# Two transformer layers on one core: the ends of pairs of query tiles start with the sums of their last exponentials

## The chip, the cores and the metric

The kernel runs on one core of one Trainium2 chip. It works with TensorE (PE), VectorE (DVE), ScalarE (ACT), GpSimd (POOL) and the DMA queue of SyncE (SP). The metric is the device time of one launch in microseconds (us), lower is better. Five runs of the kernel before gave 570.61 us in the median (563.48 to 572.50). The profile is of one other execution, which took 571.08 us.

## The reference

There are four batches of 512 tokens with 128 features, and four stages, each with a residual sum and a layer norm behind it:

```python
x = _layernorm(x + _L0_attn_ref(x, ...))   # 8 heads of 16, relative positions, softmax
x = _layernorm(x + _L0_ffn_ref(x, ...))    # 8 experts of 128->512->128, top 1, silu
x = _layernorm(x + _L1_attn_ref(x, ...))   # convolution, gates, scan over the sequence
x = _layernorm(x + _L1_ffn_ref(x, ...))    # 14 experts of 128->256->128, top 1, gelu
```

Of the first stage, this is what the change moves: the head outputs are divided by the sums of the exponentials, joined, and multiplied with Wo.

```python
attn = jax.nn.softmax(score, axis=-1)
ctx = jnp.einsum('bhqk,bkhd->bqhd', attn, v).reshape(b, s, e)
return ctx @ Wo + bo
```

The expert layers need the whole of their batches first: every token is given to the expert with the highest logit, tokens are sorted into blocks of 128 of one expert, and the blocks go through the matmuls. That sorting is done on the chip.

## The kernel before, in words

**Attention** is a list `steps` (L1327) of 64 steps (batch b, query tile t, pair of heads p), 16 to a batch. In turn k of `attention` (L1338) the scores of step k are computed (`main`, `aux`) and their row maxima taken on DVE (`nmax`); the exponentials of step k-1 (`pr`) run on ACT, which also sums them into `sums` (`exponentials`, L987); the exponentials of step k-2 are turned by PE (`ptr`) and copied by ACT (`prT`); and, in every second turn, four heads of step k-3 are multiplied with the values (`values`, L1011: `ctx`, copied to `cT`). So there are three turns behind the last scores, k = 64, 65 and 66, which only finish.

**Side work.** At the end of each turn the generators in the list `side` are advanced twice each, all of them once and then all again: the preparation of later batches (`attn_prep`), the ends of query tiles, and the first expert layer of batches 0 and 1 (`experts`, group 0). `pause(n)` (L404) lets 2n of these advances pass. `bank` (L410) makes a generator wait until the turn has a PSUM bank left for side work: `room` is 1 in turns with a `ctx`, otherwise 2. The order of instructions on every engine in this part is the order in which they are written.

**The end of two query tiles**, `tiles_end` (L1023), takes the reciprocal of the sums (`rec`), spreads it (`wide`), turns it on PE (`prr`), multiplies the head outputs with it (`cT`), multiplies with Wo on PE (`po`) and adds to the residual `xs`. It is entered into `side` in the turn in which the last `ctx` of its two tiles was issued, three turns behind their last scores. Behind the second pair of a batch, `attn_end` (L1056) takes over for the batch: moments, the reciprocal root (`rstd_b`, a power on POOL), `xf`, its transpose (`pxf`, `xfT`), the router (`pl`, `route` L524), the ranks of the tokens (`rank`, `dispatch` L606), and four indirect DMAs per batch from POOL that put the rows into `sent`. When both batches of a group are through, `experts` (L1086) fetches them (`rows`, on SP), turns them (`pxs`), and runs blocks through up matmuls (`ph`), bias and activation (`hb`, `th`) and down matmuls (`py`); the results go through DRAM (`ys`, `made`) and are gathered by POOL (`back`).

**Behind the attention** a planner takes over: `play` (L376) writes the instructions of many generators in the order in which a clock of estimated durations finds them ready, so one shift changes the order of all that follows. Where that clock sees PE idle for more than two microseconds, it puts in matmuls whose results are overwritten (L1676, `pass_time` L97). Two generators begin: `rest_of_last` (L1654), with priority, does the last `tiles_end` (batch 3, second pair) and the `attn_end` of batch 3, and then the experts of group 1 (batches 2 and 3); `rest_of_first` (L1639) finishes what is left in `side`, the `attn_end` of batch 2 and the experts of group 0. Then come the recurrences of the second layer (`pj`, `pg`, `pa`, `pgo`), its router, and its experts, first for group 0, then for group 1.

Of the kernel before, what the change touches and what calls it, by code (L numbers as in the profile page):

```python
# [19 lines left out]
B, S, D = 4, 512, 128  # L20
H, DH = 8, 16
# [177 lines left out]
def tile_kernel(ctx: ExitStack, tc: tile.TileContext, x, wpack, cols, rows, tabs, b2bd0, b2bd1,  # L199
# [37 lines left out]
    def ps(name):  # L237
        t = psum.tile([P, 512], F32, tag="any", name=name)
        clock.unread.add(clock.tile_of(t))
        clock.banks[clock.tile_of(t)] = t  # L240
        return t
# [34 lines left out]
    def col(name, i=0):  # L276
        at = _COLS[name][0] + i
        return colt[:, at : at + 1]
# [89 lines left out]
    def done():  # L368

        return clock.last  # L370
# [33 lines left out]
    def pause(n):  # L404

        if now[0] is not None:
            for _ in range(2 * n):
                yield

    def bank(*needs):  # L410
        if psum_e is not None:
            yield (*needs, common_bank)
            return
        while now[0] is not None and not room[0]:
            yield
            yield
        room[0] -= 1
# [569 lines left out]
    def exponentials(b, t, p, main, nmax):  # L987

        nm = f"{b}_{t}_{p}"
        if t % 2 == 0 and p == 0:  # L990
            sums[b, t // 2] = small.tile([P, 2, H], F32, tag="sums", bufs=2, name=f"sums{nm}")
        prs = []
        for i in range(2):
            pr = ap6.tile([P, S], F32, tag="pr", name=f"pr{nm}_{i}")
            nc.scalar.activation(pr, main[:, i, :], AF.Exp, bias=nmax[:, i : i + 1],
                                 accum_out=sums[b, t // 2][:, t % 2, 2 * p + i : 2 * p + i + 1])
            prs.append(pr)
        return prs

    def flip(b, t, h, pr):  # L1000
        nm = f"{b}_{t}_{h}"
        ptr = ps(f"ptr{nm}")
        for c in range(NT):
            nc.tensor.transpose(ptr[:, c * P : (c + 1) * P], pr[:, c * P : (c + 1) * P], ident)
        prT = ap6.tile([P, NT, P], F32, tag="prT", name=f"prT{nm}")
        nc.scalar.copy(prT.rearrange("p c q -> p (c q)"), ptr)
        return prT

    cTs, sums = {}, {}
# [13 lines left out]
    def tiles_end(b, t2):  # L1023

        nm = f"{b}_{t2}"
        cT = cTs.pop((b, t2))
        rec = small.tile([P, 2 * NG * 4], F32, tag="rec", bufs=1, name=f"rec{nm}")
        nc.vector.reciprocal(rec, sums.pop((b, t2)).rearrange("p i h -> p (i h)"))
        wide = ap2.tile([P, 2 * NG, 4, 2 * DH], F32, tag="wide", bufs=1, name=f"wide{nm}")
        nc.vector.tensor_copy(wide.rearrange("p g h d -> p (g h) d"), rec.unsqueeze(2).to_broadcast([P, 2 * NG * 4, 2 * DH]))  # L1030
        yield from pause(1)
        yield from bank(wide)
        pr_ = ps(f"prr{nm}")
        for g in range(2 * NG):
            nc.tensor.transpose(pr_[:, g * P : (g + 1) * P], wide[:, g].rearrange("p h d -> p (h d)"), ident)
        yield (done(),)
        flat = cT.rearrange("p i g q -> p (i g q)")
        nc.vector.tensor_tensor(flat, pr_, flat, ALU.mult)
        yield
        yield from bank(cT)  # L1040
        po = ps(f"po{nm}")
        for i in range(2):
            for g in range(NG):
                nc.tensor.matmul(po[:, i * D : (i + 1) * D], lhsT=cT[:, i, g, :], rhs=wwo[:, g, :],
                                 start=(g == 0), stop=(g == NG - 1))
        yield (done(),)
        mine = xs[b][:, 2 * t2 : 2 * t2 + 2, :].rearrange("p n d -> p (n d)")
        nc.vector.tensor_tensor(mine, po[:, : 2 * D], mine, ALU.add)
        if t2 == 1 and b < B - 1:
            gen = attn_end(b)  # L1050
            side.insert(0, gen)
            if b == GROUPS[0][-1]:
                urgent.append(gen)
        yield

    def attn_end(b):  # L1056

        last = b == B - 1
        x1[b] = keep.tile([P, NT, D], F32, tag="x1", name=f"x1_{b}")
        yield  # L1060
        mean, var = moments(xs[b], f"b{b}")
        rstd, both = yield from rstds_of(var, 1e-6, f"b{b}", nc.vector if last else nc.gpsimd)
        yield
        yield
        xf = keep2.tile([P, NT, D], F32, tag="xf", bufs=len(GROUPS[0]), name=f"xf{b}")
        xf_of[b] = xf
        apply_norm(xf, xs[b], mean, both, nc.vector)
        apply_norm(x1[b], xs[b], mean, rstd, nc.gpsimd)
        yield from pause(1)
        yield from bank(xf)  # L1070
        pt = transposed(xf, f"pxf{b}")
        yield (done(),)
        xfT[b] = keep2.tile([P, S], F32, tag="xfT", name=f"xfT{b}")
        nc.scalar.activation(xfT[b], pt, AF.Identity, scale=col("rms_w"))
        yield from pause(1)
        yield
        w = []
        yield from route(xfT[b], colr("gate"), E0, b, 0, w)
        if b == GROUPS[0][-1]:
            side.append(experts(0, 0, pack[0], E0, F0, "b1_0", col("rms_w")))  # L1080
        if last:
            begin(b2_of(w[0], b2t0, b, 0, x1[b], x1[b]), 1)
        else:
            yield from b2_of(w[0], b2t0, b, 0, x1[b], x1[b])
# [242 lines left out]
    steps = [(b, t, p) for b in range(B) for t in range(NT) for p in range(H // 2)]  # L1327

    side, urgent = [], []

    def advance(gens):
        for gen in list(gens):
            if next(gen, "end") == "end":
                gens.remove(gen)

    mains, probs, flipped, peaks = {}, {}, {}, {}

    def attention(first, last):  # L1338

        for k in range(first, last):  # L1340
            now[0] = k
            turning = [(*steps[k - 2], i) for i in range(2)] if 2 <= k < len(steps) + 2 else []

            def turn_one(b, t, p, i):
                flipped[b, t, 2 * p + i] = flip(b, t, 2 * p + i, probs[k - 2][i])


            if turning:
                turn_one(*turning[0])
            if k - 1 in peaks:  # L1350
                probs[k - 1] = exponentials(*peaks.pop(k - 1))
            if k < len(steps):
                mains[k] = scores(*steps[k])
                b, t, p = steps[k]
                if k == 3:
                    later_constants()
                    side.extend([turn_keys(), conv_weights(), clear_sent(), attn_prep(1), pack_weights()])
                if t == NT - 1 and p == 0 and b + 2 < B:
                    side.append(attn_prep(b + 2))
            if turning:  # L1360
                turn_one(*turning[1])
            due = None
            if 3 <= k < len(steps) + 3:
                b, t, p = steps[k - 3]
                if p % 2 == 1:
                    due = b, t, p // 2
                    values(*due, [flipped.pop((b, t, 4 * (p // 2) + i)) for i in range(4)])
            room[0] = (3 if k < 3 else 2) if due is None else 1
            if k < len(steps):
                peaks[k] = softmax(*steps[k], *mains.pop(k))  # L1370
            halves = list(side)
            advance(side)
            for gen in halves:
                if gen in side and next(gen, "end") == "end":
                    side.remove(gen)
            if due is not None and due[2] == 1 and due[1] % 2 == 1:
                side.insert(int(side[:1] == urgent), tiles_end(due[0], due[1] // 2))

    def wide_ps(name):
        if psum_e is None:  # L1380
# [273 lines left out]
    def rest_of_last():  # L1654
        last_experts = experts(1, 0, pack[0], E0, F0, "b1_0", col("rms_w"))
        next(last_experts)
        yield from tiles_end(B - 1, 1)
        yield from attn_end(B - 1)
        yield from last_experts
        load_layer1()  # L1660
        while 1 not in gxs:
            yield BLOCKED
        backs = []
        for b in GROUPS[1]:
            yield (made[0, 1], lambda: clock.free["gpsimd"])
            backs.append(gather(b, 0))
        for b, back in zip(GROUPS[1], backs):
            yield from layer0_end(b, back)
        for b in GROUPS[1]:
            while b - 2 not in over_with:  # L1670
                yield BLOCKED
            begin(recurrence(b), -1)
        yield from layer1(1)
# [114 lines left out]
```

## Time and profile before

| what | value |
|---|---|
| median of five runs | 570.61 us (563.48 to 572.50) |
| profiled execution: time, span | 571.08 us, 569.4 us |
| PE busy | 482.8 us, 85% of the span |
| DVE busy | 374.4 us, 66% |
| ACT busy | 297.5 us, 52% |
| POOL busy | 166.8 us, 29% |
| attention, from the first scores to the last `ctx` | 17.7 to 310.9 us |
| from there to the first rows of group 1 on PE | 310.9 to 349.5 us |
| recurrences and the rest of the first expert layer | 349.5 to 475.2 us |
| experts of the second layer, group 0 and then group 1 | 475.2 to 569.4 us |

Times within the span count from its first instruction. A line of the timeline reads: start, duration, engine, line, operation, tile written <- tiles read, shape, count, and in brackets the engine's idle time before it and what ended it. Nearly all operations have the line of one helper, L193, so tiles tell them apart. The profile counts two for each float32 matmul and one for each transpose, so a group written as four matmuls shows as x8 and four transposes as x4.

### The profile page before, as it was taken

The numbers are of one execution on the slowest core, as the hardware profiler recorded it, in microseconds if no ns is written. First come the engines' busy times: TensorE is split into PE (matmuls) and PEld (weight loads), VectorE is DVE, ScalarE is ACT, GpSimd is POOL, SyncE is SP. The second block draws the span as 40 slices with busy tenths as digits, with TensorE's granted clock in tenths as the row PEclk, the third lists the DMA queues.
The fourth block names the chain that finished last, engine by engine and source line by source line (L and its number), as shares of the span: only waits on it lengthen the run. The fifth ranks groups of instructions, "written<-read, shape, count | busy, mean of one in ns | idle before, by whom it ended". The sixth has DMA issues, their size and how long they took to land.

```text
span 569.4 us, 11328 instructions
## 1 busy us (share of the span) xinstructions
PE 482.8 (85%) x4076; PEld 338.6 (59%) x4076; DVE 374.4 (66%) x1033; ACT 297.5 (52%) x747; POOL 166.8 (29%) x272
## 2 busy tenths in 40 slices
PE   8988899988799888998897788999899897895930
PEld 5456465666556655676676665885445447794830
DVE  3777776776767866677573874964877586570615
ACT  1157566575655754566665121564563645573831
POOL 2484060140621402004000436313432222232533
PEclk9989999998999995699999989999999988897975
DMA  8999661330002800100328618751000017146432
GB/s 301 322 317 260 178 121 28 49 85 1 15 7 47 269 2 23 54 16 1 115 84 293 230 45 274 267 149 52 18 1 6 14 37 204 35 107 195 126 96 56
DMA packets 63848, 64.04 MB, mean 112 GB/s; under 512 B 4784, under 2 KB 53296, under 8 KB 63536
## 3 DMA queue, kind: packets, MB, share of 16 engines
q1 hardware_dynamic: 61744, 59.12, 35.6%
q0 software_dynamic: 2048, 4.20, 2.5%
q8 instruction: 32, 0.52, 0.4%
q14 instruction: 24, 0.20, 0.1%
HBM read 44.16 MB, written 20.45 MB: 113 GB/s over the span
## 4 chain that ended last, share of the span: by engine, by line
PE 53%; DVE 22%; ACT 9%; DMA 6%; issue 5%; POOL 3%; SPq 0%; ACTq 0%; DVEq 0%; POOLq 0%
PE ptr L193 8%; PE pa L193 7%; PE main L193 6%; PE ph L193 5%; PE py L193 5%; DVE nmax L193 4%; PE ctx L193 4%; DVE hb L193 4%; PE aux L193 4%; DVE main L193 3%; PE pj L193 3%; ACT pr L193 3%; ACT prT L193 2%; DMA rows<-sent 2%; PE pqa L193 1%
## 5 line engine op out<-in xcount | busy, mean ns | idle before, releaser
L193 ACT COPY prT<-ptr 128x512 f32<-128x512 f32 x128 | 74.6, 586 | 72.3 <-PE ptr L193 71.6
L193 PE MATMUL ptr<-ident,pr 128*128 128x128 f32 x512 | 86.2, 295 | 16.2 <-ACT prT L193 8.0
L193 PEld LDWEIGHTS ptr<-ident,pr 128*128 128x128 f32 x512 | 58.2, 147 | 56.1 <-ACT prT L193 17.8
L193 ACT ACTIVATE pr<-main,nmax 128x512 f32<-128x512 f32 x128 | 87.1, 689 | 6.5 <-DVE nmax L193 6.5
L193 DVE TENSOR_REDUCE nmax<-main 128x2 f32<-128x1024 f32 x64 | 78.4, 1224 | 2.2
L193 DVE COPY_PREDICATED main<-low,aux 128x256 f32<-128x256 uint32 x64 | 27.4, 428 | 64.1 <-PE aux L193 60.4
L193 PE MATMUL ph<-xt,wd 128*128 128x128 f32 x296 | 40.4, 280 | 7.9 <-ACT prT L193 4.8
L193 POOL DMA_INDIRECT back<-made,at x32 | 33.3, 1041 | 43.7 <-DMA made<-ys 23.6
L193 PE MATMUL aux<-Ko,QLo 32*128 32x128 f32 x472 | 44.5, 308 | 1.4 <-DVE mv_a L193 1.4
L193 PEld LDWEIGHTS ph<-xt,wd 128*128 128x128 f32 x296 | 36.1, 192 | 11.8 <-ACT prT L193 6.7
L193 PE MATMUL main<-KR,QR 32*128 32x512 f32 (+3 forms) x192 | 41.6, 511 | 0.0
L193 PE MATMUL ctx<-prT,V 128*32 128x128 f32 x1024 | 37.6, 292 | 4.6 <-ACT prT L193 3.8
L193 ACT ACTIVATE th<-hb 128x512 f32<-128x512 f32 x30 | 18.8, 629 | 38.7 <-DVE hb L193 36.2
L193 PEld LDWEIGHTS ctx<-prT,V 128*32 128x32 f32 x1024 | 28.0, 116 | 11.3 <-ACT prT L193 6.3
L193 PE MATMUL py<-wd,hb 128*128 128x128 f32 x248 | 32.1, 278 | 2.4 <-ACT prT L193 1.2
L193 PEld LDWEIGHTS aux<-Ko,QLo 32*128 32x128 f32 x472 | 32.9, 196 | 1.9 <-DVE mv_a L193 1.9
L193 PEld LDWEIGHTS py<-wd,hb 128*128 128x128 f32 x248 | 29.7, 192 | 5.1 <-ACT prT L193 1.6
L193 POOL DMA_INDIRECT sent<-x,at x16 | 17.2, 1072 | 47.3 <-ACT gKR L193 20.2
L193 PE MATMUL main<-K,QL 32*128 32x128 f32 (+2 forms) x192 | 29.5, 384 | 0.0
L193 POOL DMA_INDIRECT sent<-xf,at x16 | 16.3, 1016 | 43.5 <-DVE at L193 29.4
L193 DVE COPY_PREDICATED main<-ident,aux 128x256 f32<-128x256 uint32 (+1 forms) x64 | 27.4, 428 | 2.2
L193 DVE SCALAR_TENSOR_TENSOR res<-back,share,res 128x128 f32<-128x128 f32 x16 | 5.6, 351 | 34.8 <-DMA back<-made,at 34.8
(306 smaller groups left out, 991.8 us busy)
## 6 DMA issues: line engine op xcount, KB each, us to landing
wd<-pack SPq DMA_DIRECT2D x24, 512.0 KB, 5.4
wd<-pack SPq DMA_DIRECT2D x20, 256.0 KB, 3.7
pack<-in_W_dram SPq DMA_DIRECT2D x16, 256.0 KB, 5.7
rows<-sent SPq DMA_DIRECT2D x16, 256.0 KB, 3.7
made<-ys SPq DMA_DIRECT2D x16, 256.0 KB, 2.5
pack<-in_W_dram SPq DMA_DIRECT2D x28, 128.0 KB, 3.2
sent<-zero SPq DMA_DIRECT2D x2, 1344.0 KB, 11.0
tab<-in_tabs_dram SPq DMA_DIRECT2D x2, 1280.0 KB, 9.4
```

What stands on the lines that cost most here:

```text
L193: return inner(*args, **kw)
```

## The change

`tiles_end` is entered into `side` two turns earlier: at the end of the turn in which the exponentials of its last step were issued (k - 1), when `sums` is complete but the last `prT` and `ctx` are not. Its pause grows by one turn, and the head outputs are taken from `cTs` behind the pause. So `rec` and `wide` move two turns forward, `prr`, `po` and all that follows one turn. For batch 0's first pair it goes to the end of the list (it stands behind the preparation of batch 1), otherwise to its front as before. In the turns 64 to 66 only generators named `tiles_end` are advanced; the rest of `side` waits for the planner. `rest_of_last` takes up the last `tiles_end` where it stands in `side`, instead of beginning a new one.

```diff
     def tiles_end(b, t2):
         nm = f"{b}_{t2}"
-        cT = cTs.pop((b, t2))
         rec = small.tile([P, 2 * NG * 4], F32, tag="rec", bufs=1, name=f"rec{nm}")
...
-        yield from pause(1)
+        yield from pause(2)
+        cT = cTs.pop((b, t2))
         yield from bank(wide)
...
-    def advance(gens):
-        for gen in list(gens):
-            if next(gen, "end") == "end":
-                gens.remove(gen)
...
-            halves = list(side)
-            advance(side)
-            for gen in halves:
+
+            halves = [gen for gen in side if k < len(steps) or gen.__name__ == "tiles_end"]
+            for gen in (*halves, *halves):
                 if gen in side and next(gen, "end") == "end":
                     side.remove(gen)
-            if due is not None and due[2] == 1 and due[1] % 2 == 1:
-                side.insert(int(side[:1] == urgent), tiles_end(due[0], due[1] // 2))
+
+            if 1 <= k <= len(steps) and steps[k - 1][1] % 2 == 1 and steps[k - 1][2] == H // 2 - 1:
+                b, t, _ = steps[k - 1]
+                side.insert(len(side) if b == 0 and t == 1 else int(side[:1] == urgent), tiles_end(b, t // 2))
...
-        yield from tiles_end(B - 1, 1)
+        for gen in side:
+            if gen.__name__ == "tiles_end":
+                yield from gen
         yield from attn_end(B - 1)
```

## The prediction

> **What bounds the kernel now.** I read the page first (busy shares and the clock row), then the windows, then PE's timeline behind the attention, then the chain of waits. PE is busy 85% of the span, but the stages differ. In the attention a plain pair of turns takes 5.36 us (3.21 with a `ctx`, 2.15 without): ACT alone needs 5.0 of it (four `pr` at 0.69, four `prT` at 0.57). From 350 to 463 us PE has work nearly all the time: its named waits there sum to 7 us. Between lies this stretch, from PE's timeline (start, duration, tile, idle time before it):
>
> ```profile
> 312.78 0.66 PE L193 MATMUL prr<-ident,wide 128*128 128x128 f32 x4 [0.35 <-DVE hb L193]
> ...
> 322.77 0.60 PE L193 MATMUL pxf<-ident,xf 128*128 128x128 f32 x4
> ...
> 329.48 0.96 PE L193 MATMUL pl<-colt,xfT 128*128 128x8 f32 x8
> ...
> 333.90 0.36 PE L193 MATMUL rank<-before,ones 128*128 128x8 f32 x2 [0.67 <-DVE sm L193]
> ...
> 337.25 11.02 PE L1676 MATMUL pxs<-b2t,ident 128*128 128x512 f32 x18 [0.90 <-DVE farther L193]
> 349.51 0.66 PE L193 MATMUL pxs<-ident,rows 128*128 128x128 f32 x4 [1.24 <-DMA rows<-sent]
> ```
>
> These are batch 3's own steps; all group 1 waits for them. The last `ctx` ends at about 310.84. From there to the first rows of group 1, 38.7 us pass, and 12.3 of them (337.25 to 349.51) hold on PE only filler matmuls and idle time. The chain of waits names the end of it:
>
> ```profile
> 342.41 4.06 DMA sent<-xf,at
> 346.49 2.98 DMA rows<-sent
> 349.51 0.67 PE pxs L193 x4
> ```
>
> The second place is the clock. The windows (span, then busy us of PE, PEld, DVE, ACT, POOL, then granted clock) show a half clock that covers 213.6 to 237.5 us:
>
> ```profile
> 209.00:212.00 3.00, 2.12 (x19) 1.83 (x16) 2.76 (x7) 1.16 (x4) 0.00 (x0) 1.00 0.00 0
> 215.00:218.00 3.00, 2.21 (x34) 1.66 (x35) 2.73 (x13) 0.61 (x2) 0.00 (x0) 0.50 0.00 0
> ...
> 233.00:236.00 3.00, 3.00 (x9) 1.81 (x10) 2.71 (x6) 0.59 (x1) 0.00 (x0) 0.50 0.00 0
> 239.00:242.00 3.00, 3.00 (x50) 2.11 (x43) 1.88 (x3) 2.25 (x6) 0.00 (x0) 1.00 0.01 3
> ```
>
> Four turns take 24.0 us there (212.5 to 236.5); the same four of the batch before took 18.9 with 2.8 us more side work on PE. So this stretch costs 5 to 8 us, and five runs of one program that spread by 9 us may differ by just that.
>
> **The change part by part.**
>
> *Ends of tiles inside the attention.* Nothing is added or removed. `prr` (0.5 us issue) leaves a turn with `ctx` for one without, `po` (0.9) the reverse. A turn with `ctx` and `prr` takes 3.71, so +0.5 over plain; one with `po` and 1.1 of other work 4.41, +2.26 over 2.15 for 2.0 of work. The swap costs nothing to within 0.3 us for each of seven ends, so -2 to +2 in all; I take 0. `rec` and `wide` (0.25 + 0.43 on DVE) move ahead of two turns; the sums are there, since ACT issued those exponentials a turn before. DVE queues the next turn's masks and `nmax` behind them as it does now. POOL's clears of `V` and `QR` for a later batch and SP's copies of `QL` and `K` move by a turn or two, with ten turns to spare.
>
> *Group 0's experts start two turns earlier* (first `pxs` before turn 51, then 49), since batch 1's end comes earlier. By the order of instructions, one up, two downs and one `pxs` more then lie before the end of turn 63: 0.9 + 1.8 + 0.3 = 3.0 us of PE work. The twelve turns 51 to 62 took 55.6 us where plain ones take 32.2, for 14.65 us of side matmuls, so side work costs 1.6 us for each us on PE. That makes +4.8.
>
> *The last three turns* lose one up, `pxs`, two downs, and an up behind the last `ctx`. They took 10.6 us (300.25 to 310.84). What is left: `ptr` 0.6, `prT` 0.6, four `pr` pieces 1.35, `prT` 0.5, `ctx` 1.05, `cT` 0.3, `ptr` 0.7, two `prT` 1.05, 0.6 of hand-overs to PE: 6.8. So -3.8. The attention ends at +1.0 (from -1 if the early experts hide in ACT's shadow, to +2.5).
>
> *Batch 3's chain*, in us from the end of the last `ctx`, before in brackets. `prr` 0 (1.94: it stood behind an up and `pxf`, and waited for `hb`). `cT` times `prr` done at 1.45, `po` ends 2.6, `xs` starts 2.65 (5.28: DVE did batch 2's routing first). Moments take 1.74 as now: 4.4; the power on POOL 1.66: 6.15. Meanwhile DVE routes batch 2 (1.9 + 0.55), until 6.9; then root 0.82, `xf` 1.12: 8.85 (11.72). `pxf` and `xfT`: 10.4. `pl` follows at once, 11.4 (it ends at 19.6 now, because `xfT` stood on ACT behind a `th`, then `pl` on PE behind ups and downs). DVE then has batch 2's dispatch 2.3, `x` 0.6, `hb` 0.6 and 0.65, so `mx` starts at 13.1 and ends its group at 15.0 (22.8). `rank` 15.2 to 15.9. Ahead of the dispatch DVE has four `hb` pieces and the shares: 18.1; its 3.44 us end at 21.55 (27.36). Gain 5.8. POOL: the four `x` (3.31) now precede batch 2's four `sent` (5.0), 7.75 to 16.3, then the clear of `w` by 16.5; DVE needs that `w` at 16.75, so it is covered by a quarter of a us only. From dispatch to rows I keep the 11.2 us of now; on SP nothing that waits longer stands ahead of the rows. First rows of group 1: 349.5 + 1.0 - 5.8 = 344.7, a gain of 4.8 (bounds 2.3 to 7).
>
> *Behind it* the planner's order decides. Group 0's last results come 2.3 us later (its last activations stand behind the 4.15 us of block sums on DVE), but PE has `ph` and `py` of group 1 to do meanwhile. Counted from the first rows of group 1, PE's work until the first `pxs` of the second layer is 4.3 us more: five fillers at 0.86 (one before `pgx`, one before `pb`, three before `pa`). They cost nothing if PE waits there, 4.3 if not. Now it waits 5.8 us for exactly that `pxs` (469.3 to 475.2). I take half, +2.2. From `pgo` of batch 3 to its `rank`, 13.6 us of PE work instead of 14.9: -1.0. Sum: -4.8 + 2.2 - 1.0 = -3.6, bounds -8 (nothing lost) to +1.8 (attention +2.5, chain -5, fillers +4.3). The tail behind is the same.
>
> **A rule that speaks against it.** Row first: PE idled 1.66 us before the `ptr` at 126.61, and the clock fell to 0.5 until about 132. In the new order I find PE without work and without filler from about 22.5 to 27.9 us behind the last `ctx`: `py` needs activations that stand behind the block sums. The Trainium skill, "TensorE: Matmul & The Clock Gate", Part 1, says that an idle window of some 3.4 us halves the clock and a busy one of that length restores it. By that rule the first 3.4 us of group 1 cost an estimated 1.7 us. By the row, 4 us at half cost 2; by the stretch at 213 us, 24.
>
> **The rivals.** *Half clock gone*: the stretch at 213 us doesn't come up in the shifted order (-5 to -8 on top): 558 to 563. For it: batch 0's same turns ran at full clock. Against: the same work still meets there, DVE as loaded. *Nothing gained*: group 1's rows come earlier, but fillers and side work take it back: 570 to 574. For it: PE is nearly full from 350 to 463, and only waits can be saved. *Slower*: the gap of 5.4 us starts a half clock in the stage from 345 us, where PE was busy 18.8 of 20 us, so every us at half costs 0.5. It decides from 7 us on; lasting 24 us, as at 213, it costs 12: 571.1 - 3.6 + 12 = 579. Against it: PE's work there is dense, at 213 it had gaps.
>
> **How the numbers follow.** The sum is made against the profiled execution: 571.08 - 3.6 = 567.5; the median of 570.61 lies 0.5 lower, so 567. Chances: forecast (564 to 570) 0.50; half clock gone 0.17; nothing gained 0.20; slower 0.13. The range from 559 to 574 holds the forecast, the second rival, and most of the first. Faster by over 2% (below 559.2) is the better half of the first rival: 0.09. Slower by over 2% (above 582) is the worst third of the last: 0.05. Two per cent is about what a measurement of this kernel can tell from no change.
>
> **What would show it.** Right: last `ctx` within 1 us of 311; `prr` right behind it; `pl` of batch 3 some 11 us and `rank` 15 us behind it instead of 19 and 23; no 11 us of fillers before `pxs`, which starts near 345; `pxs` of the second layer near 472. Wrong: an attention that ends over 3 us later, a `w` that DVE waits for, a clock of 0.5 over more than two windows behind 345, or a half clock at 213 that came or went.

## The result, and the profile after

The changed kernel takes 569.45 us in the median (564.78 to 576.18), the kernel before 570.03 (560.70 to 577.68). The ratio of undisturbed runs is 1.0049, 95% interval 1.0028 to 1.0070: half a per cent slower, 2.8 us, where 3.6 us of gain were forecast. (That ratio leaves out runs over 1.5% above the fastest of the same kernel, which is why it is not the quotient of the medians; over all runs the medians agree to 0.1%.) The profiled execution took 569.0 us, its span is 567.3 us.

The page of the changed kernel, first part: busy us, share of the span, and instructions of each engine.

```profile
PE 473.7 (83%) x4070; PEld 334.5 (59%) x4070; DVE 376.3 (66%) x1033; ACT 298.3 (53%) x747; POOL 172.0 (30%) x272
```

PE was busy for 9 us less than before, and yet nothing was gained. PE's timeline of the changed kernel behind the attention (start, duration, operation, tile written <- tiles read, shape, count, idle time before it and what ended it):

```profile
308.66 1.55 PE L193 MATMUL ctx<-prT,V 128*32 128x128 f32 x32 [0.29 <-ACT prT L193]
310.14 0.66 PE L193 MATMUL prr<-ident,wide 128*128 128x128 f32 x4
...
321.11 0.95 PE L193 MATMUL pl<-colt,xfT 128*128 128x8 f32 x8
...
325.64 0.39 PE L193 MATMUL rank<-before,ones 128*128 128x8 f32 x2
...
336.90 6.24 PE L193 MATMUL py<-wd,hb 128*128 128x128 f32 x24 [2.62 <-DVE hb L193]
343.55 0.63 PE L193 MATMUL pxs<-ident,rows 128*128 128x128 f32 x4 [0.41 <-DMA rows<-sent]
```

Batch 3's chain does what was forecast. `prr` stands right behind the last `ctx` (end 310.21), `pl` follows 10.9 us behind it (forecast 10.4 to 11.4), `rank` 15.4 (forecast 15.2). The 11 us of fillers before `pxs` are gone. The first rows of group 1 come 33.3 us behind the last `ctx` instead of 38.6, a gain of 5.3 against a forecast 5.8.

Where the time went is therefore ahead of this stretch or behind it. The windows (span, then busy us of PE, PEld, DVE, ACT, POOL, then granted clock, DMA share, GB/s) show first that the clock hides it:

```profile
209.00:212.00 3.00, 2.27 (x36) 1.71 (x34) 2.76 (x9) 0.59 (x1) 0.00 (x0) 0.50 0.00 0
212.00:215.00 3.00, 2.61 (x18) 2.22 (x11) 2.16 (x14) 0.27 (x1) 0.38 (x1) 0.50 0.00 0
...
337.00:340.00 3.00, 3.00 (x13) 2.73 (x14) 2.34 (x4) 1.31 (x3) 0.69 (x1) 0.50 0.74 247
340.00:343.00 3.00, 2.94 (x13) 2.51 (x12) 0.69 (x1) 0.61 (x2) 0.00 (x0) 0.50 0.38 113
```

In this execution the half clock in the middle of the attention covers some 10 us (207 to 217), in that of before it covered 24. So the last `ctx` ends at almost the same time (310.2 and 310.9), although, as the next part shows, the attention's work has become longer. A single pair of executions can't be read here without the clock.

**A ruler for the attention.** Where the order of instructions up to a turn is the same and the clock full, most turns from 9 on have the same duration in every execution to about 0.02 us. Four executions have the order of before up to turn 62 (before, and the experiments e3, e5, e7), and five that of the changed kernel (after, e1, e2, e4, e6), with half clock partly in different turns. The shortest duration of each turn in its family is taken as the turn at full clock (sums of the unrounded turns, in us):

| turns | order of before | order of after | difference |
|---|---|---|---|
| 9 to 16 | 33.4 | 33.6 | +0.2 |
| 17 to 25 | 36.3 | 37.7 | +1.4 |
| 26 to 35 | 46.6 | 46.0 | -0.6 |
| 36 to 46 | 43.3 | 47.6 | +4.3 |
| 47 to 50 | 14.7 | 14.0 | -0.7 |
| 51 to 62 | 55.3 | 59.8 | +4.6 |
| 9 to 62 | 229.5 | 238.8 | +9.2 |
| start of 63 to the last `ctx` | 15.0 | 11.4 | -3.6 |

The attention is 5.6 us longer, not 1.0. Two places of the ruler are rough. Turn 26 has at least 3.4 us at half clock in all four executions with the order of before, so its 5.7 us are not at full clock, and the loss in the turns up to 46 is more likely larger than smaller. And the shortest turns from 47 to 62 never came together in one execution of the order of before: e7, at full clock there throughout, took 71.4 us for them where the changed kernel took 74.7, which is +3.4 instead of the +3.8 of the table. What a microsecond of half clock costs follows from the same turns: those of before took 238.4 in its profiled execution with 27.3 us at half clock, so 0.32 us each; those of after took 243.3 with 10.2 us, so 0.45.

### The profile page after: what moved, and what is told of

Same layout as the page of the kernel before. It is cut to its first block, busy times and chain, and to the rows that moved or that the text cites. A ratio compares the mean times of both kernels' runs of the same rounds, so it can differ in the third digit from the quotient of the medians.

```text
span 567.3 us, 11323 instructions
## 1 busy us (share of the span) xinstructions
PE 473.7 (83%) x4070; PEld 334.5 (59%) x4070; DVE 376.3 (66%) x1033; ACT 298.3 (53%) x747; POOL 172.0 (30%) x272
## 5 line engine op out<-in xcount | busy, mean ns | idle before, releaser
L193 PE MATMUL ptr<-ident,pr 128*128 128x128 f32 x512 | 82.7, 285 | 16.7 <-ACT prT L193 6.7
L193 PEld LDWEIGHTS ptr<-ident,pr 128*128 128x128 f32 x512 | 56.1, 142 | 55.0 <-ACT prT L193 19.9
L193 DVE COPY_PREDICATED main<-low,aux 128x256 f32<-128x256 uint32 x64 | 27.3, 427 | 61.3 <-PE aux L193 57.6
L193 POOL DMA_INDIRECT back<-made,at x32 | 33.3, 1040 | 43.9 <-DMA made<-ys 23.4
L193 PE MATMUL ctx<-prT,V 128*32 128x128 f32 x1024 | 35.9, 280 | 10.0 <-ACT prT L193 8.7
L193 PE MATMUL aux<-Ko,QLo 32*128 32x128 f32 x472 | 43.0, 300 | 0.8 <-DVE st_a L193 0.8
L193 PE MATMUL py<-wd,hb 128*128 128x128 f32 x248 | 35.2, 292 | 5.1 <-DVE hb L193 2.6
L193 PE MATMUL main<-KR,QR 32*128 32x512 f32 (+3 forms) x192 | 39.3, 486 | 0.0
L193 PEld LDWEIGHTS py<-wd,hb 128*128 128x128 f32 x248 | 32.3, 205 | 8.1 <-DVE hb L193 3.7
L193 PEld LDWEIGHTS ctx<-prT,V 128*32 128x32 f32 x1024 | 26.7, 111 | 16.9 <-ACT prT L193 12.4
L193 POOL TENSOR_TENSOR QL<-QL,t 128x512 f32<-128x512 f32 x8 | 10.2, 1270 | 60.5 <-DVE t L193 60.5
L193 ACT ACTIVATE ys<-py 128x128 f32<-128x128 f32 (+1 forms) x65 | 19.0, 293 | 17.5 <-PE py L193 15.3
```

What stands on the lines that cost most here:

```text
L193: return inner(*args, **kw)
```

## The experiments

Each ran on one chip together with the kernel before. The first four were on one chip (before: 576.39 us in the median), e5 to e8 on a second (568.13), e9 and e10 on a third (570.70). Two theories carry the study: A, that the loss sits in the planner's order behind the attention, and C, that the earlier ends and experts lengthen the attention itself. (B, in the first expectations, is that the gain was never there and only the half clock differed.)

### e1: batch 1's dispatch in the second layer held back

Behind the first rows of group 1, the second layer's first `pxs` came 131.7 us later in the changed kernel and 125.6 in the one before. In its trace PE waits 2.71 us for DVE's `gKo` (until 462.22), which stands behind batch 1's dispatch:

```profile
462.22 4.54 PE L193 MATMUL pa<-gKo,wabct 128*128 128x512 f32 x6 [2.71 <-DVE gKo L193]
```

The edit makes that dispatch wait for batch 3's `u`:

```diff
+        while layer == 1 and b == 1 and 3 not in u_ready:
+            yield BLOCKED
```

> The changed kernel, but batch 1's dispatch in the second layer is not planned before the u of batch 3 stands. Theory A (the 6 us that the chain of batch 3 wins are lost because DVE has 7 us of batch 1's dispatch ahead of batch 3's second u, so that pa of batch 3 starts at 462 us): pa of batch 3 runs without the wait of 2.7 us and without the three fillers, the first rows of the second layer come near 471 us instead of 475, and the time is 3 to 5 us below the changed kernel, 562 to 566 us. Theory B (the 6 us were never there: only the half clock in the attention was shorter in that execution): the same as the changed kernel within 1.5 us.

Measured: 578.56 us (573.58 to 586.34), ratio 0.9996 (0.9965 to 1.0028). The wait for `gKo` falls to 0.55 us:

```profile
469.09 2.84 PE L193 MATMUL pa<-gKo,wabct 128*128 128x512 f32 x6 [0.55 <-DVE gKo L193]
```

From the first rows of group 1 to the second layer's `pxs` it is still 130.1 us. So by the traces that wait is worth 1.6 us at most, and most of the longer stage stays. How much of it reaches the end is open: the ratio would allow the whole loss to be gone, the medians (578.56 and 576.39) would not, and the changed kernel itself was not run on this chip.

### e2: the early ends alone

The changed kernel, but all of `side` goes on in the last three turns:

```diff
-            halves = [gen for gen in side if k < len(steps) or gen.__name__ == "tiles_end"]
+            halves = list(side)
```

> Only the earlier entry of the ends of tiles: in the last three turns all of the side work goes on as before the change. Theory A: the last ctx ends 3 to 4 us later than in the changed kernel (313 to 314 us), the chain behind it keeps most of its gain, the first rows of group 1 on PE come near 346 to 348 us; the total depends on the order that the planner finds, within 4 us of the kernel before. Theory B: first rows of group 1 at 350 us or later.

Measured: 589.23 us (582.84 to 590.18), ratio 1.0181 (1.0131 to 1.0232). From the start of turn 63 to the last `ctx` it takes 15.57 us instead of 11.42. The early ends by themselves lose; the shorter last turns belong to the other half of the change. From the second layer's first `pxs` to the end it also takes 99.1 us, against 92.1 in the changed kernel; that was not followed.

### e3: the last turns alone

The kernel before, with nothing of `side` advanced in the turns 64 to 66:

```diff
-            halves = list(side)
-            advance(side)
-            for gen in halves:
+            halves = list(side) if k < len(steps) else []
+            for gen in (*halves, *halves):
```

> Only the second part: ends of tiles enter where they did, but nothing of the side goes on in the last three turns. Theory A: the last ctx ends 3 to 4 us earlier than in the kernel before, near 307 us; rec and wide still stand behind the last ctx, so prr comes about 1 us behind it; first rows of group 1 near 343 to 346 us; total again by the planner's order, within 4 us of the kernel before. Theory B: first rows of group 1 not before 348 us.

Measured: 575.46 us (568.73 to 583.99), ratio 0.9978 (0.9934 to 1.0022). Turn 63 to the last `ctx` takes 11.28 us instead of 15.02, but the first rows of group 1 come 42.3 us behind it instead of 38.6 (41.1 in e5). What the heads gain, the chain gives back. Batch 3's `prr` now stands 0.4 us behind the last `ctx` (1.9 before), but its `pl` ends 20.7 us behind it (19.5 before), after ups and downs on PE. That this is the work taken out of the last turns is likely and not shown.

### e4: no fillers

The changed kernel without the planner's fillers, whose results nobody reads:

```diff
-        for _ in range(int((self.starts("tensor", out, ins) - self.free["tensor"] - 2.0) / takes)):
+        for _ in range(0):
```

> The changed kernel without the filler matmuls (their results are overwritten, nothing is left out of the result). If fillers cost 0.86 us each, as the prediction's upper bound had it, the time falls by 3 to 4 us. If they stand in waits that end elsewhere (Theory A: on DVE's queue), it stays within 1 us, or rises by 1 to 3 us where the clock falls to half in the gaps that they filled.

Measured: 590.28 us (581.01 to 601.97), ratio 1.0101 (1.0035 to 1.0167): slower than the kernel before; whether it is also slower than the changed kernel (1.0028 to 1.0070) the intervals leave open. Its windows behind the last `ctx` (311.0):

```profile
314.00:318.00 4.00, 1.06 (x8) 1.00 (x7) 3.62 (x26) 0.23 (x1) 1.66 (x1) 0.69 0.99 334
318.00:322.00 4.00, 2.87 (x10) 1.98 (x11) 3.55 (x17) 0.95 (x2) 3.26 (x4) 0.50 0.22 80
322.00:326.00 4.00, 4.00 (x16) 3.16 (x15) 1.40 (x3) 0.00 (x0) 2.99 (x3) 0.50 0.11 37
```

The same windows of the changed kernel, with fillers at 313.45 and 317.81:

```profile
314.00:318.00 4.00, 3.46 (x14) 1.73 (x13) 3.51 (x26) 0.49 (x2) 1.94 (x2) 1.00 0.87 310
318.00:322.00 4.00, 3.22 (x17) 1.98 (x16) 3.66 (x17) 0.69 (x1) 3.36 (x5) 1.00 0.01 3
322.00:326.00 4.00, 4.00 (x37) 3.91 (x36) 3.27 (x14) 0.75 (x2) 3.09 (x4) 1.00 0.16 47
```

With PE busy 1.06 of 4 us the clock falls to 0.5 and stays there while PE is busy again. With 3.46 of 4 it stays at 1.00. Between the last `ctx` and group 1's rows, 18.5 us run at half clock instead of 6.8. So the fillers, of which the prediction took half as a loss, are not where the time went: without them nothing is gained.

### e5 and e6: both kernels again

The kernel before and the changed kernel, unchanged, beside e7 and e8.

> The kernel before itself, for a profile on the same chip as the next three: ratio 1.00 within 0.005. By the turns at full clock in the runs so far, its last ctx ends near 297 us plus 0.45 us for every us at half clock ahead of it, and the first rows of group 1 follow 35 to 39 us later.

> The changed kernel itself on the same chip. Theory C (the ends of tiles that stand one turn earlier cost the attention some 7 us at full clock, besides the packed experts' 4.5, because the moments and the routing of DVE and po now share their turns with ctx; the chain of batch 3 gives 5 back; the rest is as before): last ctx near 305.5 us plus 0.45 us per us at half clock, first rows of group 1 33 us later, in the full-clock sum 4 to 6 us slower than the kernel before. Theory A (attention unchanged, gain lost in the planner's order): last ctx within 2 us of the kernel before at equal half clock.

Measured: e5 569.33 us, ratio 0.9978 (0.9903 to 1.0053); e6 569.82 us, ratio 1.0072 (1.0039 to 1.0104). The loss is there on another chip too. By luck these two profiled executions had the same half clock in the attention (13.7 us in both), so they can be compared stage by stage:

| stage (us) | e5, before | e6, after | difference |
|---|---|---|---|
| first scores to the last `ctx` | 287.2 | 293.5 | +6.2 |
| to the first rows of group 1 | 41.1 | 33.3 | -7.8 |
| to the second layer's first `pxs` | 127.5 | 131.2 | +3.8 |
| to the end | 94.1 | 92.5 | -1.6 |

The ruler gave +5.6 for the first row. (In the second, 7.7 and 4.0 us are at half clock; the first pair of executions, with 6.8 in both, gives -5.3.)

### e7: only the last end early

The kernel before, with the changed kernel's last three turns, and only batch 3's last `tiles_end` entered early:

```diff
+            if k == len(steps):
+                side.insert(0, tiles_end(B - 1, 1, 2))
-            if due is not None and due[2] == 1 and due[1] % 2 == 1:
+            if due is not None and due[2] == 1 and due[1] % 2 == 1 and k < len(steps):
```

(with the pause as the third argument, two turns here and one elsewhere, and `rest_of_last` as in the changed kernel).

> Only the very last end of tiles enters two turns earlier, all others where they stood before the change; the last three turns as in the change. Theory C: the attention up to turn 63 is that of the kernel before to the hundredth, the last ctx comes 4 us earlier than there, prr right behind it, the first rows of group 1 33 us behind it, so 8 to 9 us earlier than in the kernel before; the time falls by 4 to 9 us (ratio 0.984 to 0.993). Theory A: first rows as early, but the gain is lost behind, ratio 0.997 to 1.005.

Measured: 556.13 us (554.70 to 564.18), ratio 0.9832 (0.9781 to 0.9882). This beats both kernels. PE's timeline of e7 around the end of the attention:

```profile
303.12 1.55 PE L193 MATMUL ctx<-prT,V 128*32 128x128 f32 x32 [0.29 <-ACT prT L193]
304.60 0.66 PE L193 MATMUL prr<-ident,wide 128*128 128x128 f32 x4
...
315.56 0.95 PE L193 MATMUL pl<-colt,xfT 128*128 128x8 f32 x8
...
320.35 0.29 PE L193 MATMUL rank<-before,ones 128*128 128x8 f32 x2
...
338.59 0.66 PE L193 MATMUL pxs<-ident,rows 128*128 128x128 f32 x4 [0.46 <-DMA rows<-sent]
```

`prr`, `pl` and `rank` stand 0, 10.9 and 15.7 us behind the last `ctx`, as in the changed kernel, and the rows 33.9. So the whole gain of the chain comes from this one end and the three last turns. Turns 0 to 62 are those of before.

### e8: all ends entered early, but their matmuls where they were

The changed kernel with one more turn of pause in `tiles_end`, so that `prr` and `po` return to the turns they had before (except for the first pair of batch 0, which stays at the end of the list):

```diff
-        yield from pause(2)
+        yield from pause(3)
```

> The changed kernel with a pause of three turns instead of two: rec and wide keep their early place, but prr, po and the end of each batch stand in the turns where they stood before the change. Theory C: turns 17 to 62 take what they take in the kernel before at full clock, within 2 us in the sum, and the time is that of the run with only the last end early, within 2 us; the changed kernel is 5 us or more slower than this. Theory A: as the changed kernel within 2 us.

Measured: 558.60 us (556.48 to 562.60), ratio 0.9879 (0.9832 to 0.9925). From turn 36 to turn 46 it takes 43.3 us, as before, and 11.28 us from the start of turn 63 to the last `ctx`. One turn more of pause is worth some 1.9% (0.9879 against e6's 1.0072 on the same chip). Entering an end early costs nothing that the intervals of e7 and e8 can tell; running it a turn earlier does. Theory C holds for the attention, but that is not all of it: from the first rows of group 1 to the second layer's first `pxs` e7 takes 125.5 us and e8 126.7, like the kernel before (125.6 and 127.5), while the changed kernel takes 131.7 and 131.2 and e10, below, 131.5. So the earlier end of batch 1 lengthens that stage too (the stage behind it is 0.3 to 1.9 us shorter in return). The planner writes it, so this is Theory A's part; which instruction costs it was not followed.

### e9 and e10: which of the ends costs

e10 keeps only the end of batch 1's second pair a turn earlier (and with it batch 1's routing and group 0's experts). e9 does the opposite: all the others earlier, that one not.

```diff
-        yield from pause(2)
+        yield from pause(3 if (b, t2) == (1, 1) else 2)
```

(e9; e10 has 2 and 3 exchanged.)

> The changed kernel, with a pause of three turns only in the end of batch 1's second pair: the other ends stay one turn earlier (prr beside no ctx, po beside one), but the routing of batch 1 and the experts of group 0 start where they did in the kernel before. With all pauses at three turns the ratio was 0.9879. Theory D1 (each moved end costs on its own, some 5 us in all in turns 9 to 46): those turns take 164 us at full clock instead of 159.5, turns 51 to 62 stay at 55.3; ratio 0.995 to 0.999. Theory D2 (the cost comes from batch 1's routing two turns earlier, which meets the moved ends in turns 43 and 44, and from the early experts): turns 9 to 46 take 160 to 161.5 us, turns 51 to 62 55.3; ratio 0.988 to 0.992. Rival (the loss is the planner's order behind the attention, not the turns): ratio as the changed kernel's, 1.005.

> The changed kernel with pauses of three turns in all ends but that of batch 1's second pair: only this end is earlier than before, and with it batch 1's routing and the experts of group 0. D1: turns 9 to 46 take 160 us, turns 51 to 62 59.8 (the experts' 4.5 us); ratio 0.995 to 0.998. D2: turns 9 to 46 already take 162 to 164, turns 51 to 62 59.8; ratio 1.000 to 1.005, nearly the changed kernel's. Rival (planner's order): 0.988 or 1.005, with turns as before.

Measured: e10 563.79 us (561.22 to 570.79), ratio 0.9997 (0.9934 to 1.0061), an interval too wide to part D1 from D2. Its turns speak for D2 up to turn 46: 47.0 us in turns 26 to 35, then 48.5 in turns 36 to 46 and 58.5 in turns 51 to 62, where before has 46.6, 43.3 and 55.3. From turn 36 on this was at full clock, as the windows of e10 show:

```profile
175.00:205.00 30.00, 25.36 (x338) 18.44 (x334) 21.38 (x52) 18.72 (x49) 7.93 (x15) 1.00 0.41 93
205.00:225.00 20.00, 15.26 (x198) 10.34 (x193) 14.73 (x46) 11.73 (x31) 4.03 (x4) 1.00 0.37 132
225.00:297.00 72.00, 64.40 (x784) 49.02 (x784) 51.98 (x95) 46.43 (x117) 6.62 (x11) 1.00 0.17 54
```

So the earlier end of batch 1 alone brings +5.3 in turns 36 to 46, more than the +4.3 of the whole change, and in turns 51 to 62 +2.1 against e7's 56.4 at full clock.

e9: 578.11 us (574.91 to 583.10), ratio 1.0291 (1.0159 to 1.0423), slower than everything expected of it. Turns 17 to 25 take 37.7 us as in the changed kernel, turns 36 to 46 45.8 (partly at half clock), but turns 51 to 62 take 66.3 instead of 55.3; 6.8 us there are at half clock, worth some 3. Both D1 and D2 had these turns unchanged. Turn 53 shows what happens there. In e7 it holds the `po` of batch 2's second pair and one group of up matmuls (`ph`), and the `ptr` behind them does not wait. In e9 that `po` has moved to turn 52, two groups of `ph` stand in turn 53, and the `ptr` waits for DVE to read them:

```profile
253.97 0.66 PE L193 MATMUL ptr<-ident,pr 128*128 128x128 f32 x4 [1.34 <-DVE hb L193]
```

Turns 55, 57 and 61 show the same. The costs don't add: what a moved end costs depends on which side work shares its turn. e9 is also some 5 us longer behind the second layer's first `pxs` (97.4 against 92.1 in the changed kernel); that was not followed.

## Why the prediction was wrong

The forecast moved in the wrong direction, mainly by one term.

**"The swap costs nothing to within 0.3 us for each of seven ends, so -2 to +2 in all; I take 0."** This step failed: turns 9 to 46 became 5.4 us longer (159.5 and 164.9, the sum of the ruler's first four rows). The step priced `prr` and `po` by PE time in otherwise plain turns. It had no term for what moves with them: batch 1's end brings `attn_end` of batch 1 forward by a turn, `route` and `dispatch` by two, and there these stand on DVE in front of what PE waits for. It is plainest in turns 43 and 44, where the routing meets the end of batch 2's first pair. e1 ran them at full clock. PE's timeline of e1, turns 43 and 44:

```profile
213.77 0.60 PE L193 MATMUL prr<-ident,wide 128*128 128x128 f32 x4
214.84 0.39 PE L193 MATMUL rank<-before,ones 128*128 128x8 f32 x2 [0.47 <-ACT prT L193]
...
216.84 0.66 PE L193 MATMUL ptr<-ident,pr 128*128 128x128 f32 x4 [1.14 <-DVE cT L193]
...
221.51 1.16 PE L193 MATMUL po<-wwo,cT 128*128 128x128 f32 x8 [0.39 <-ACT cT L193]
223.16 0.66 PE L193 MATMUL ptr<-ident,pr 128*128 128x128 f32 x4 [0.49 <-DVE farther L193]
```

DVE's timeline of e1 in the same turns:

```profile
215.57 0.17 DVE L193 TENSOR_REDUCE sm<-ex 128x4 f32<-128x32 f32 x1
...
216.10 0.68 DVE L193 TENSOR_TENSOR cT<-prr,cT 128x512 f32<-128x512 f32 x1
...
220.78 0.21 DVE L193 TENSOR_TENSOR more<-rank,over 128x56 f32<-128x56 f32 x1
...
223.14 0.19 DVE L193 TENSOR_TENSOR farther<-farther,jump 128x32 f32<-128x32 f32 x1
```

The kernel gives `ptr`, `prr`, `po` and `rank` two banks between them (L225). The next `ptr` needs a bank that `prr` or `rank` holds until DVE has read it: at 216.84 it waits for `cT`, which stands behind the batch's shares, at 223.16 for the last reads of `rank` at the end of the dispatch. ACT's `prT` waits for that `ptr`, its timeline says how long:

```profile
217.59 0.58 ACT L193 COPY prT<-ptr 128x512 f32<-128x512 f32 x1 [2.80 <-PE ptr L193]
...
223.91 0.58 ACT L193 COPY prT<-ptr 128x512 f32<-128x512 f32 x1 [2.45 <-PE ptr L193]
```

Turn 43 takes 5.20 us instead of 3.21, turn 44 6.32 instead of 4.28. Before, the same `prr` met no routing in its turn (PE's timeline of e5, turns 44 and 45):

```profile
206.12 0.66 PE L193 MATMUL prr<-ident,wide 128*128 128x128 f32 x4 [0.52 <-ACT prT L193]
...
208.71 1.05 PE L193 MATMUL po<-wwo,cT 128*128 128x128 f32 x8
209.76 0.39 PE L193 MATMUL rank<-before,ones 128*128 128x8 f32 x2
...
211.50 0.66 PE L193 MATMUL ptr<-ident,pr 128*128 128x128 f32 x4 [0.88 <-DVE xs L193]
```

There the shares cost turn 45 a wait of 0.88 us instead, and turn 45 took 4.94 us; in the changed kernel it takes 3.21. So of the 4.0 us that turns 43 and 44 gain in length, 2.3 are a net loss. Another 2.0 stand in turns 36 to 42, above all in turns 39 and 40 (3.27 and 5.10 us instead of 2.15 and 4.38), where batch 1's `xf` and its transpose `pxf` now stand with the preparation of batch 3 (`V`). PE's timeline of e6, turns 39 and 40, at full clock:

```profile
188.40 0.66 PE L193 MATMUL pxf<-ident,xf 128*128 128x128 f32 x4 [0.52 <-DVE V L193]
...
192.48 1.08 PE L193 MATMUL ctx<-prT,V 128*32 128x128 f32 x32 [1.33 <-ACT prT L193]
```

and the same `ctx` in e5, which does not wait:

```profile
189.57 1.08 PE L193 MATMUL ctx<-prT,V 128*32 128x128 f32 x32
```

The +1.4 us of turns 17 to 25, where batch 0's end stands, were not followed. The prediction moved group 0's experts with batch 1's end, but not the routing in front of them. e10 shows that this one end suffices for the whole loss in turns 36 to 46 (there above all in turns 37 and 44, 5.77 and 6.31 us instead of 4.41 and 4.28); e8 shows that it goes when `prr` and `po` go back.

The other steps, in the prediction's order:

| step | forecast (us) | measured (us) | from |
|---|---|---|---|
| ends swapped between turns | 0 (-2 to +2) | +5.4 | turns 9 to 46 |
| group 0's experts two turns earlier | +4.8 | +3.8; +3.4 | turns 47 to 62: the ruler; against e7 |
| last three turns | -3.8 | -3.6 | start of 63 to the last `ctx` |
| attention as a whole | +1.0 (-1 to +2.5) | +5.6; +6.2 | the ruler; e5 and e6 |
| batch 3's chain | -5.8 | -5.3; -7.8 | before and after; e5 and e6 |
| behind the first rows | +1.2 | +3.9; +2.2 | before and after; e5 and e6 |
| sum | -3.6 | +2.8 | ratio 1.0049 |

The sum by the ruler and the first pair of executions is 5.6 - 5.3 + 3.9 = +4.2, by e5 and e6 6.2 - 7.8 + 2.2 = +0.6; the measured +2.8 lies between. Without the failed step the first would be -1.2, the second -4.8.

Right, or near it, were the price of the earlier experts (forecast 4.8, measured 3.4 to 3.8), the three last turns, and the chain almost to the instruction: the clear of `w` on POOL, which I had covered by a quarter of a microsecond, in fact held DVE up for 0.19. Behind the first rows, the mechanism was right but the term too small: PE waits for DVE's `gKo` there, which e1 prices at 1.6 at most; what makes up the rest of that stage is open. The fillers were counted as half a loss; e4 shows that nothing is gained without them.

The rule that spoke against the change (the Trainium skill, "TensorE: Matmul & The Clock Gate", Part 1) was put in the right place: the gap came (2.62 us idle ahead of the `py` at 336.90, at 26.7 us behind the last `ctx`), and the clock was at half from about 337 to 343. The gap that the profile shows is shorter than the 3.4 us that the page names, as is the 1.66 us of the prediction's row. But before has 6.8 us of half clock in its stretch too, so the change neither gained nor lost by it. The rival that would have made the kernel slower, a long half clock from this gap, did not happen. The rival of a half clock gone at 213 us looked true in the one profiled execution and is not: other executions of the same order have long ones.

## What to carry to other kernels

Before work is moved by one turn, list everything that is started by its end, and look on every engine at what each of these instructions will stand in front of in its new turn; here the matmuls cost little by themselves, and the routing that came with them held the banks that the next transposes needed. Where only one end sets the path, move only that one: e7 takes the chain's whole gain and leaves the other turns alone. Where a clock comes and goes between executions, compare stages by turns of the same order, not by the ends of two traces.

## What the runs showed of the hardware

**Half clock comes and goes between executions of one program.** Two executions of the kernel before had 30.7 and 13.7 us at half clock up to the last `ctx`. The changed kernel, e1 and e4 have the same instructions up to turn 62, but 10.2, 34.1 and 10.2 us at half clock up to the last `ctx`, which ended at 310.2, 321.1 and 311.0. In turns 9 to 62 a microsecond at half clock cost 0.32 to 0.37 us in the four executions with the order of before, and 0.44 to 0.51 in the five with that of the changed kernel. Not all of it comes and goes: turn 26 had at least 3.4 us of it in all four executions with the order of before.

**A busy PE does not bring the full clock back at once.** In the changed kernel's windows at 209 and 212 PE was busy 2.27 and 2.61 of 3 us, and the clock still was 0.50; in e4 PE worked without a gap from 321.3 us on, and the clock came back at 329.2, 7.9 us later. By the rule of the Trainium skill ("TensorE: Matmul & The Clock Gate", Part 1) a busy window of 3.4 us would restore the clock; in the trace of before it stayed at half for 24 us with PE busy for 2.1 to 3.0 us of every 3. What ends a half clock here stays open.
